# A preln attention and FP4 feed-forward kernel: the down projection one step later, two key blocks joined in one, other orders at both ends

## The chip, the cores and the metric

The kernel runs on one core of a Trainium2 chip. The time is what the device needs for one execution, in microseconds; a kernel's time is the median of its runs. Beside the runs there is one profiled execution, from which all rows come. Engines: PE is TensorE, PEld its weight loads, DVE is VectorE, ACT is ScalarE, POOL is GpSimd, SP issues most DMAs.

## The reference

Eight sequences of 2048 rows with 256 features go through one block of a transformer, all in fp32:

```python
x = x + attention(layernorm(x), W_Q, W_K, W_V)
x = x + ffn(layernorm(x), w_gate, w_up, w_down)

# attention: Q = xpos(X @ W_Q); K = xpos(X @ W_K, downscale=True); V = X @ W_V
p = softmax(Q @ K.T, axis=-1) * 0.9 ** abs(n - m)
out = p @ V
# ffn (704 hidden features); every operand of a product is rounded to FP4
# in blocks of 16, with a scale of max(abs(block)) / 6
h = silu(fp4(x) @ fp4(w_gate).T) * (fp4(x) @ fp4(w_up).T)
out = fp4(h) @ fp4(w_down).T
```

The softmax runs over all 2048 keys. The decay makes what is far from the diagonal negligible, so the kernel multiplies only a band of keys with V.

## The kernel before

**Tiles.** A row block has 128 rows. There are 16 to a sequence (NB) and 128 in all (`total`). Four row blocks are a group: it is normalised, turned, and projected to K, Q and V at a time (`project_rotated`, `rotate`, `project_v`, `keep_v`). The four groups of the first sequence are projected ahead of the steps, all others during the steps of the sequence before.

**Attention of a row block.** `scores` makes two tiles `s` of 1024 keys each in PSUM; `maximum` and `exponentials` make the softmax's numerators. `turn_p` transposes those of the band: VectorE transposes squares of 32, ScalarE's queue issues a DMA to DRAM (`there_p`), SP's queue issues four DMAs back (`runs`). `decays` multiplies by the decay on VectorE, four key blocks of 128 keys at a time, into `p_t`, and `attend` multiplies with V, one matmul for each key block. The band reaches BAND = 7 blocks to either side, so a row block has 8 to 15 key blocks. The matmuls are in fp32, and the profile lists each as two passes.

**Feed-forward of a row block.** `add_residual` and `normal_scales` make `xq`, the FP4 rounding of the rows (`Fp4.largest`, `normalize`, `round`). Its wide operations go to POOL unless `wide_on` says otherwise. `turn_xq` and `keep_xq` turn it into `xq_t`, `gate_up` multiplies, `hidden` makes `h`, which is rounded in the same way. `turn_h` (by DRAM, as above; in the last four blocks by TensorE) and `keep_h` (a ScalarE copy) turn it into `h_t`, `down` multiplies with w_down's columns into `d`, and `finish` adds and writes out.

**Order.** The program is written out by hand: each engine's queue and SP's run in the order in which `step(n)` calls these functions. In step n stand the scores of block n, `attend` of n-1, `xq` and `gate_up` of n-2, `h` of n-3 and the down part of n-4. So `keep_h(n-4)` and `down(n-4)` are in the same step, and `h_t` has one buffer. The tiles `s`, `gate`, `up`, `pp_*`, `pv` and most `pt_*` share three PSUM buffers; `d`, `o` and `pt_xq` share two.

**Both ends.** FFN weights are rounded and turned inside the early steps, by the table `IN_STEPS` (`round_weights`, `turn_ffn_weights`); key "r" is what w_gate and w_up have beyond 512 rows, ("d", 0) and ("d", 1) are the halves of w_down. Near the end the blocks in `deferred` (120 to 122) leave out their `down`; it runs among the last chains, where little else is left. In those steps `decays_first` puts `decays` ahead. After step 127 the last chains of `h` are written out by hand.

Of the kernel before, what the change touches and what calls it, by code (L numbers as in the profile page):

```python
# [34 lines left out]
def preln_xpos_retention_fp4_ffn_kernel(  # L35
# [89 lines left out]
    make_identity(nc, ident)  # L125
    neg_half = cpool.tile([P, BPG], F32, name="neg_half")
# [20 lines left out]
    load_pair("k", w_k)  # L147
    load_group(1)
# [17 lines left out]
    class Fp4:  # L166
# [37 lines left out]
        def round(self, wide_on=None):  # L204
# [19 lines left out]
            wide_on = wide_on or self.wide_on  # L224
            wide_on.tensor_tensor(v, v, big, ALU.add)  # L225
            wide_on.tensor_tensor(v, v, big, ALU.subtract)  # L226
            wide_on.tensor_tensor(self.v3, self.v3, self.wide(self.scale), ALU.mult)
# [108 lines left out]
    def round_weights(key):  # L336
        weight_fp4[key].round(nc.vector if key == ("d", 1) else None)
# [7 lines left out]
        (1, "residual"): [(round_weights, "r")],  # L345
        (2, "decays"): [(round_weights, ("d", 0)), (round_weights, ("d", 1))],
        (2, "attend"): [(turn_ffn_weights, "r")],
        (3, "maximum"): [(turn_ffn_weights, ("d", 0))],
        (3, "attend"): [(turn_ffn_weights, ("d", 1))],
# [10 lines left out]
    def statistics(k, blocks=range(BPG)):  # L360
        xt, n = groups[k], len(blocks)
        mv = small.tile([P, BPG, 2], F32, tag="mv4", bufs=2, name=f"mv_{k}_{blocks[0]}")
        for j, c in enumerate(blocks):
            st = small.tile([P, 6], F32, tag="st", name=f"st_{k}_{c}")
            nc.vector.bn_stats(st, xt[:, c, :])
            nc.vector.bn_aggr(mv[:, j, :], st)
        normed[k, blocks] = (mv, layernorm_scale(mv, n, f"a{k}_{blocks[0]}"))
# [60 lines left out]
    def rotate(k, name):  # L428
# [4 lines left out]
        for half in range(2):  # L433
            rot = act_p.tile([P, GROUP], F32, tag="rot", bufs=2, name=f"rot_{name}{half}_{k}")
# [30 lines left out]

    deferred = {n: None for n in range(total - 8, total - 5)}
# [76 lines left out]

    def decays(n):
        keys, pt = band(n), turned[n]
        p_t = prob_p.tile([P, 2 * BAND + 1, P], F32, tag="p_t", bufs=1, name=f"p_t_{n}")
        d0 = keys[0] - n % NB + BAND
        for c in range(0, len(keys), BPG):  # L550
            to = min(c + BPG, len(keys))
            nc.vector.tensor_tensor(  # L552
                p_t[:, c:to, :].rearrange("p k (a i) -> p k a i", a=NSQ),
                pt[:, c:to],
                decay_sb[:, d0 + c : d0 + to, :].rearrange("p k (a i) -> p k a i", a=NSQ),
                ALU.mult,
            )
# [4 lines left out]
    def attend(n):  # L562
# [3 lines left out]
        for j, k in enumerate(keys):  # L566
            nc.tensor.matmul(  # L567
                po,
                p_t[:, j, :],
                vt[b, k // BPG][:, k % BPG, :],  # L570
                start=(j == 0),
                stop=(j == len(keys) - 1),
            )
# [7 lines left out]
    def add_residual(n):  # L581
        if n in deferred:
            deferred[n] = act_p.tile([P, 2 * GROUP], F32, tag="kt", bufs=2 * NG, name=f"deferred_{n}")
            x1 = deferred[n][:, FC * P : FC * P + H]
        else:
            x1 = ffn_p.tile([P, H], F32, tag="x1", bufs=5, name=f"x1_{n}")
# [41 lines left out]
    def gate_up(n):  # L628
        x1, xq_t = mid.pop(n)
        pss = []  # L630
        for what, w in (("gate", wg_t), ("up", wu_t)):
            ps = ps_s.tile([P, 2, GROUP], F32, tag="s", name=f"{what}_{n}")
            for hc in range(HC):
                for half in range(2):
                    nc.tensor.matmul(  # L635
                        ps[:, half, :FH],
                        xq_t[:, hc, :],
                        w[:, hc, ts(half, FH)],
                        start=(hc == 0),
                        stop=(hc == HC - 1),  # L640
                    )
# [8 lines left out]
    def hidden(n):  # L650
# [3 lines left out]
        hid[n] = (x1, h, Fp4(h, P, F, f"h{n}", wide_on=nc.vector if n == total - 1 else None))  # L654


    def turn_h(n):
        h = hid[n][1]
        if n >= total - 4:
            pt = ps_s.tile([P, FC + 2, P], F32, tag="s", name=f"pt_h_{n}")[:, :FC, :]  # L660
            for fc in range(FC):
                at = min(fc * P, F - P)
                nc.tensor.transpose(pt[:, fc, :], h[:, at : at + P], ident)  # L663
            keep_h(n, pt.rearrange("p c (a i) -> p c a i", a=NSQ))
# [3 lines left out]
    def keep_h(n, src=None):  # L668
        x1, h, _ = hid[n]
        if n in deferred:  # L670
            h_t = deferred[n][:, : FC * P].rearrange("p (c q) -> p c q", c=FC)
        else:
            h_t = ffn_p.tile([P, FC, P], F32, tag="h_t", bufs=1, name=f"h_t_{n}")
        nc.scalar.copy(  # L674
            h_t.rearrange("p c (a i) -> p c a i", a=NSQ), in_runs(h) if src is None else src
        )
        hid[n] = (x1, h_t)

    def down(n):
        x1, h_t = hid.pop(n)  # L680
# [14 lines left out]
    hold_ffn_weights()  # L695
    load_ffn_weights("g")
    load_tables()
    load_pair("q", w_q)
# [6 lines left out]
    turn_x(0)  # L705
    load_tables()
# [4 lines left out]
    separate("q")  # L711
    for g in range(NG):
# [8 lines left out]
        if g == 0:  # L721
# [9 lines left out]
            nc.sync.dma_start(decay_sb, decay)  # L731
        if g + 1 < NG:
            project_v(g)
            keep_v(g)
        if g == 0:
            normalize_on_scalar(3)
        if g == 1:
            scale_weights("r")
            round_weights("g")

    kept = []

    def decays_first(n):

        return n - 4 in deferred

    def step(n):
# [5 lines left out]
        if on(3):  # L753
            hidden(n - 3)
        if on(2):
# [3 lines left out]
        maximum(n, 0)  # L759
        weights_in_step(n, "maximum")  # L760
        scores(n, 1)
        if decays_first(n):
            turn_xq(n - 2)
            decays(n - 1)
        if on(3):
            hid[n - 3][2].normalize()
        if on(4) and n - 4 < total - 4:
            keep_h(n - 4)
        if decays_first(n):
# [181 lines left out]
```

## Time and profile before

| | us |
|---|---|
| median of 3 runs | 2883.12 |
| lowest and highest | 2882.41, 2883.24 |
| profiled execution | 2880.51 |
| its span, first to last instruction | 2878.7 |
| PE busy | 2820.6 |
| DVE busy | 2465.1 |
| POOL busy | 1417.4 |
| ACT busy | 1077.9 |

A row of the profile's groups names the line of the kernel, the engine, the operation, and what it writes and reads, with the count; after the bar stand the busy time of the group and the mean length of one in nanoseconds; after the second bar the idle time of the engine just before such an instruction, and what ended most of it. Matmuls overlap, so the mean of one is longer than what it adds. In a timeline row the first two numbers are start and length, "xN" the number of passes, and a bracket names the idle time before and what ended it. In a list of waits the three numbers are the total, the count and the longest.

### The profile page before, as it was taken

The page shows a single profiled execution, that of the slowest core. Times are in us where ns is not written, and L with a number is a line of the kernel's source. Part 1 is how long each engine was busy: PE and PEld are TensorE (multiplying, and loading weights), DVE is VectorE, ACT ScalarE, POOL GpSimd, SP SyncE. Part 2 cuts the span into 40 slices and gives each one's busy share as a digit, 9 for nine tenths or more (in the row PEclk, how much of TensorE's full clock was granted, in tenths as well). Part 3 has the DMA queues.
Part 4 walks back from the last instruction along what each step waited for, and adds up shares of the span by engine and source line. Part 5 has one row for each costly group of instructions (what it writes and reads, how often), then busy time and mean ns, then how long its engine had stood idle before and what let it go on. Part 6 is the DMA issues. An engine that isn't in the chain of part 4 may idle for free. (4 is left out here: it accounts for less than half of the span.)

```text
span 2878.7 us, 34636 instructions
## 1 busy us (share of the span) xinstructions
PE 2820.6 (98%) x9702; PEld 1835.8 (64%) x9702; DVE 2465.1 (86%) x5635; ACT 1077.9 (37%) x1665; POOL 1417.4 (49%) x1330
## 2 busy tenths in 40 slices
PE   8899999999999999999999999999999999999997
PEld 5466666666666666666666666666666666666655
DVE  7898888888888888888888888888888888888877
ACT  3243333333433434433443334343334433333331
POOL 6544545444555454554455445544555444544443
PEclk9899999999999999999999999999999999999999
DMA  5355544555455555455546554555554555345441
GB/s 189 116 159 165 170 147 139 177 174 160 143 160 167 165 158 155 150 164 170 163 143 174 163 159 149 161 154 167 156 164 149 171 167 157 116 135 153 150 124 38
DMA packets 365761, 441.97 MB, mean 154 GB/s; under 512 B 102784, under 2 KB 313088, under 8 KB 365568
## 3 DMA queue, kind: packets, MB, share of 16 engines
q1 hardware_dynamic: 307248, 263.84, 34.4%
q10 hardware_dynamic: 58320, 175.92, 16.2%
q8 instruction: 76, 1.25, 0.2%
q14 instruction: 117, 0.96, 0.1%
HBM read 246.94 MB, written 192.68 MB: 153 GB/s over the span
## 5 line engine op out<-in xcount | busy, mean ns | idle before, releaser
L479 PE MATMUL s<-kt,qt 128*128 128x512 f32 x2048 | 901.2, 592 | 4.4 <-ACT h L647 3.7
L479 PEld LDWEIGHTS s<-kt,qt 128*128 128x128 f32 x2048 | 388.3, 190 | 461.4 <-issue 422.1
L567 PE MATMUL o<-v,p_t 128*128 128x256 f32 x2944 | 659.9, 380 | 7.0 <-DVE p_t L552 7.0
L567 PEld LDWEIGHTS o<-v,p_t 128*128 128x128 f32 x2944 | 560.9, 191 | 88.3 <-DVE p_t L552 11.3
L225 POOL TENSOR_TENSOR h<-h,big_h 128x704 f32<-128x704 f32 x127 | 214.5, 1689 | 534.0 <-DVE big_h L223 533.8
L647 ACT ACT_TABLE_LOAD x126 | 161.7, 1283 | 727.5 <-DVE xq L599 472.2
L674 ACT COPY h_t<-h 128x768 f32<-128x768 f32 x121 | 100.7, 832 | 756.3 <-DMA h<-there_h 696.4
L683 PE MATMUL d<-wd_t,h_t 128*128 128x256 f32 x1500 | 350.3, 383 | 17.5 <-ACT h_t L674 16.7
L491 DVE TENSOR_REDUCE m<-s 128x1 f32<-128x1024 f32 x256 | 310.4, 1212 | 52.5 <-PE s L479 51.2
L683 PEld LDWEIGHTS d<-wd_t,h_t 128*128 128x128 f32 x1500 | 282.9, 191 | 97.3 <-ACT h_t L674 38.3
L635 PE MATMUL gate<-wg_t,xq_t 128*128 128x352 f32 x1024 | 324.4, 460 | 1.6 <-ACT xq_t L621 1.6
L635 PE MATMUL up<-wu_t,xq_t 128*128 128x352 f32 x1024 | 324.2, 459 | 0.3 <-DVE rot_k L436 0.3
L512 ACT ACTIVATE p<-s,nmax 128x1024 f32<-128x1024 f32 x256 | 283.0, 1110 | 16.5 <-DVE nmax L496 15.0
L199 POOL TENSOR_TENSOR h<-h,inv_h 128x704 f32<-128x704 f32 x127 | 176.2, 1387 | 224.8 <-DVE inv_h L197 157.1
L635 PEld LDWEIGHTS up<-wu_t,xq_t 128*128 128x128 f32 x1024 | 194.2, 190 | 109.8 <-ACT p L512 1.3
L199 POOL TENSOR_TENSOR xq<-xq,inv_x 128x256 f32<-128x256 f32 x127 | 79.0, 622 | 359.8 <-DVE inv_x L197 116.4
L635 PEld LDWEIGHTS gate<-wg_t,xq_t 128*128 128x128 f32 x1024 | 194.0, 190 | 91.6 <-ACT xq_t L621 3.6
L552 DVE TENSOR_TENSOR p_t<-runs,decay_sb 128x512 f32<-128x512 f32 (+3 forms) x414 | 239.7, 636 | 3.1 <-issue 0.4
L243 DVE STREAM_TRANSPOSE sq_p<-p 128x1024 f32<-128x1024 f32 (+7 forms) x239 | 224.2, 973 | 10.2 <-ACT p L512 10.2
L226 POOL TENSOR_TENSOR h<-h,big_h 128x704 f32<-128x704 f32 x127 | 213.8, 1683 | 10.0
L512 ACT ACT_TABLE_LOAD x125 | 160.4, 1283 | 114.0 <-DVE nmax L496 90.3
L225 POOL TENSOR_TENSOR xq<-xq,big_x 128x256 f32<-128x256 f32 x127 | 92.3, 727 | 197.2 <-DVE big_x L223 197.2
(167 smaller groups left out, 3501.8 us busy)
## 6 DMA issues: line engine op xcount, KB each, us to landing
there_h<-sq_h ACTq DMA_DIRECT2D x124, 384.0 KB, 4.5
h<-there_h SPq DMA_DIRECT2D x496, 96.0 KB, 2.3
rope_k<-in_rope_dram SPq DMA_DIRECT2D x32, 512.0 KB, 5.8
rope_q<-in_rope_dram SPq DMA_DIRECT2D x32, 512.0 KB, 6.0
xr<-in_L_attn_X_dram SPq DMA_DIRECT2D x128, 128.0 KB, 2.2
there_xq<-sq_xq ACTq DMA_DIRECT2D x126, 128.0 KB, 1.7
xq<-there_xq SPq DMA_DIRECT2D x504, 32.0 KB, 1.7
out_dram<-x SPq DMA_DIRECT2D x125, 128.0 KB, 5.3
```

Of the source, the lines that this page charges most:

```text
L199: self.wide_on.tensor_tensor(self.v3, self.v3, self.wide(inv), ALU.mult)
L225: wide_on.tensor_tensor(v, v, big, ALU.add)
L226: wide_on.tensor_tensor(v, v, big, ALU.subtract)
L243: nc.vector.transpose(sq[:, :, at : at + w].rearrange("p c (k i) -> p k c i", i=SQ), src.rearrange("p (k c i) -> p k c i", c=NSQ, i=SQ),)
L479: nc.tensor.matmul(ps[:, j, :], q[:, dc, ts(i % BPG, P)], kt[b, half * 2 + j][:, dc, :], start=(dc == 0), stop=(dc == 1),)
L491: nc.vector.tensor_reduce(raw_scores[n][:, half : half + 1], raw_scores[n, half], AX.XY, ALU.max)
L512: nc.scalar.activation(pr, raw_scores.pop((n, half)).rearrange("p j k -> p (j k)"), AF.Exp, bias=nmax, accum_out=sums[:, half : half + 1],)
L552: nc.vector.tensor_tensor(p_t[:, c:to, :].rearrange("p k (a i) -> p k a i", a=NSQ), pt[:, c:to], decay_sb[:, d0 + c : d0 + to, :].rearrang ...
L567: nc.tensor.matmul(po, p_t[:, j, :], vt[b, k // BPG][:, k % BPG, :], start=(j == 0), stop=(j == len(keys) - 1),)
L635: nc.tensor.matmul(ps[:, half, :FH], xq_t[:, hc, :], w[:, hc, ts(half, FH)], start=(hc == 0), stop=(hc == HC - 1),)
L647: nc.scalar.activation(h[:, :F].rearrange("p (j f) -> p j f", j=2), pss[0], AF.Silu)
L683: nc.tensor.matmul(pd, h_t[:, fc, :], wd_t[:, fc, :], start=(fc == 0), stop=(fc == FC - 1))
```

## The change

Six things change together.

1. `down` and `finish` move from block n-4 to block n-5, and `h_t` gets two buffers. `keep_h(n-4)` stays in step n, but moves behind the exponentials and `keep_xq`. The deferred blocks and `decays_first` go: all blocks take the regular order.
2. Where the band has all 15 key blocks (`whole`: two row blocks in a sequence), only the lower half of its first key block and the upper half of its last are used. Their two halves are put in one block: `join_values` copies the halves of V on ScalarE, `decays` multiplies the halves of `p` into one block, and `attend` makes 14 matmuls instead of 15.
3. The program begins with 24 transposes of the identity on TensorE, into a tile that nobody reads. W_Q's load is issued earlier. Some of the normalisation of groups 3 and 4 and the rounding of w_gate change places.
4. Steps 0 to 5 are rearranged: "r" is rounded in step 2, w_down's halves are rounded in steps 3 and 4 (before, both in step 2) and turned in steps 4 and 5; step 2's projections come before "r" is turned; the second half's wide operations go to POOL instead of VectorE.
5. In the last 14 steps (`late`) `gate_up` is issued ahead of `turn_h`.
6. The last chains have another order; the wide operations on `h` of the last three blocks, not only of the last, are on VectorE; the last `h` is scaled and turned in two pieces.

```diff
+    idle = ps_s.tile([P, HALF, P], F32, tag="s", name="idle")
+    for j in range(3 * HALF):
+        nc.tensor.transpose(idle[:, j % HALF, :], ident, ident)
...
     load_pair("k", w_k)
+    load_pair("q", w_q)
     load_group(1)
...
-        weight_fp4[key].round(nc.vector if key == ("d", 1) else None)
+        weight_fp4[key].round()
...
-        (1, "residual"): [(round_weights, "r")],
-        (2, "decays"): [(round_weights, ("d", 0)), (round_weights, ("d", 1))],
+        (2, "maximum"): [(round_weights, "r")],
         (2, "attend"): [(turn_ffn_weights, "r")],
-        (3, "maximum"): [(turn_ffn_weights, ("d", 0))],
-        (3, "attend"): [(turn_ffn_weights, ("d", 1))],
+        (3, "maximum"): [(round_weights, ("d", 0))],
+        (4, "maximum"): [(turn_ffn_weights, ("d", 0))],
+        (4, "exponentials"): [(round_weights, ("d", 1))],
+        (5, "maximum"): [(turn_ffn_weights, ("d", 1))],
...
+    def whole(n):
+        return BAND <= n % NB < NB - BAND
+
+    def join_values(n):
+        b, i = divmod(n, NB)
+        v = small.tile([P, H], F32, tag="v_ends", bufs=1, name=f"v_ends_{n}")
+        for k, half in ((i - BAND, slice(P // 2, P)), (i + BAND, slice(0, P // 2))):
+            nc.scalar.copy(v[half], vt[b, k // BPG][half, k % BPG, :])
+        ends_of[n] = v
...
+        if whole(n):
+            decay_blocks(p_t, pt, 0, 0, 1, -BAND, slice(P // 2, P))
+            decay_blocks(p_t, pt, 0, 2 * BAND, 1, BAND, slice(0, P // 2))
...
+        values = [(j, vt[b, k // BPG][:, k % BPG, :]) for j, k in enumerate(keys)]
+        if whole(n):
+            values = values[1:-1] + [(0, ends_of.pop(n))]
...
-        hid[n] = (x1, h, Fp4(h, P, F, f"h{n}", wide_on=nc.vector if n == total - 1 else None))
+        hid[n] = (x1, h, Fp4(h, P, F, f"h{n}", wide_on=nc.vector if n >= total - 3 else None))
...
-            h_t = ffn_p.tile([P, FC, P], F32, tag="h_t", bufs=1, name=f"h_t_{n}")
+            h_t = ffn_p.tile([P, FC, P], F32, tag="h_t", name=f"h_t_{n}")
...
 def step(n):
...
-        if on(4) and n - 4 < total - 4:
-            keep_h(n - 4)
...
         maximum(n, 1)
         exponentials(n)
+        if n == 0:
+            normalize_on_scalar(NG)
...
+        if on(2):
             keep_xq(n - 2)
+        if on(4):
+            keep_h(n - 4)
...
-        if on(1) and n != 2 and not decays_first(n):
+        if on(1) and n not in (2, 3):
             decays(n - 1)
...
-        if on(4) and n - 4 not in deferred:
-            down(n - 4)
+        if on(5):
+            down(n - 5)
         if n == 2:
             attend(n - 1)
+            project()
             weights_in_step(n, "attend")
-            project()
...
+        if whole(n):
+            join_values(n)
...
-        if on(4) and n - 4 not in deferred:
-            finish(n - 4)
+        if on(5):
+            finish(n - 5)
...
+        late = n > total - NB + 1
+        if late:
+            gate_up(n - 2)
         if on(3) and n < total - 1:
             turn_h(n - 3)
...
-        if n == 1:
+        if n in (1, 2):
             decays(n)
...
-        if on(2):
+        if on(2) and not late:
             gate_up(n - 2)
```

The chains behind step 127, after the change (z = 127):

```python
add_residual(z); turn_h(z - 3); finish(z - 4); mid[z - 1][2].round(); turn_xq(z - 1)
normal_scales(z); mid[z][2].round(); gate_up(z - 1); hidden(z - 2); turn_xq(z); down(z - 3)
hid[z - 2][2].largest(); hid[z - 2][2].normalize(); gate_up(z); hid[z - 2][2].round()
turn_h(z - 2); hidden(z - 1); finish(z - 3)
hid[z - 1][2].largest(); hid[z - 1][2].normalize(); down(z - 2); hid[z - 1][2].round()
turn_h(z - 1); finish(z - 2); hidden(z); hid[z][2].largest(); hid[z][2].normalize(); down(z - 1)
half = FC // 2 * P // QBLK
hid[z][2].round(pieces=[slice(0, half), slice(half, F // QBLK)])
finish(z - 1); turn_h(z); down(z); finish(z)
```

## The prediction

> **What bounds the kernel now.** I read the page first, then TensorE's waits, then its timeline where it idles.
>
> ```profile
> span 2878.7 us, 34636 instructions
> PE 2820.6 (98%) x9702; PEld 1835.8 (64%) x9702; DVE 2465.1 (86%) x5635; ACT 1077.9 (37%) x1665; POOL 1417.4 (49%) x1330
> L567 PE MATMUL o<-v,p_t 128*128 128x256 f32 x2944 | 659.9, 380 | 7.0 <-DVE p_t L552 7.0
> L683 PE MATMUL d<-wd_t,h_t 128*128 128x256 f32 x1500 | 350.3, 383 | 17.5 <-ACT h_t L674 16.7
> ```
>
> TensorE is the bound: it lacks 58.1 us of the span. Passes overlap, so one costs busy time over count: an `o` pass 659.9/2944 = 0.224 us, a block's twelve `d` passes 2.6 us.
>
> ```profile
> PE d L683 <- ACT h_t L674: 16.7, 23, 2.5
> PE pp_k L417 <- ACT p L512: 7.9, 1, 7.9
> PE pt_h L663 <- POOL h L227: 7.4, 1, 7.4
> PE o L567 <- DVE p_t L552: 7.0, 4, 3.5
> PE pt_x L392 <- DVE x L372: 6.2, 1, 6.2
> PE s L479 <- ACT h L647: 3.7, 3, 1.2
> ```
>
> These waits (total, times, longest) are nearly all there is to win, apart from passes at a low clock:
>
> ```profile
> 9.46 5.72 PE L417 MATMUL pp_k<-xnt,wk_pair 128*128 128x512 f32 x8 [1.16 <-ACT xnt L394]
> 32.20 3.70 PE L417 MATMUL pp_k<-xnt,wk_pair 128*128 128x512 f32 x8 [1.49 <-ACT xnt L394]
> 96.22 6.71 PE L417 MATMUL pp_k<-xnt,wk_pair 128*128 128x512 f32 x8 [7.89 <-ACT p L512]
> 123.78 7.44 PE L567 MATMUL o<-v,p_t 128*128 128x256 f32 x20 [3.50 <-DVE p_t L552]
> 2793.34 4.58 PE L567 MATMUL o<-v,p_t 128*128 128x256 f32 x20 [1.64 <-DVE p_t L552]
> 2863.52 1.54 PE L663 MATMUL pt_h<-ident,h 128*128 128x128 f32 x6 [7.40 <-POOL h L227]
> 2866.01 5.07 PE L683 MATMUL d<-wd_t,h_t 128*128 128x256 f32 x12 [0.94 <-ACT h_t L674]
> ```
>
> Eight projection passes take 3.60 or 3.70 us when warm, but 5.72 at the start and 6.71 after a 7.89 us gap; twenty `o` passes 4.58, but 7.44 after 3.50. So a long gap is paid again: 2.1 + 3.1 + 2.9 us. After gaps of 1.2 to 1.7 nothing is lost. The busy times by stretch (TensorE, weight loads, VectorE, ScalarE, POOL, then the granted clock) say the same:
>
> ```profile
> 90.00:100.00 10.00, 3.78 (x5) 1.72 (x6) 8.52 (x12) 4.83 (x11) 5.22 (x5) 0.60 0.23 68
> 120.00:130.00 10.00, 6.50 (x17) 5.00 (x17) 7.95 (x18) 4.29 (x7) 4.57 (x3) 0.66 0.20 68
> ```
>
> **Joined blocks.** `whole(n)` holds at two of 16 row blocks of a sequence, 16 in all; each loses one key block, two passes: 16 x 2 x 0.224 = 7.2 us off TensorE. VectorE: three key blocks in a 384-wide multiply (0.550) become a 128-wide one (0.324) and two on 64 partitions, at most 0.324 each: +0.42 a time, beside TensorE's longest steps. ScalarE gets two copies of 64x256 (nearest, the 128x256 `xq_t` copy: 0.398), 0.8 us at 37% load. Behind them stand `there_h`'s issue and the silu, but both already come after the `attend` that the second join waits for. Bounds: 7.2 if covered, 16 x 0.8 - 7.2 = 5.6 lost if ScalarE's copies stood on the path. I take 7.2 won.
>
> **Down one step later.** 19 of the 23 waits lie in regular steps: eleven before 2450 us (5.4 us) and eight between 2560 and 2720 (6.1). The copy `keep_h` (0.83) still runs in step n, now behind the exponentials and `xq_t`, and `d` of that block is wanted a step later, so these vanish. What is late next is `p_t`: around 2607 its multiplies end at 2609.6 and `o` begins at 2609.8; without the wait TensorE would be there at 2608.7, when the first of three is done. I take 10.0 of 11.5 (bounds 4 and 11.5). On SP, `finish` stands where it was, writing one block older.
>
> **First steps.** Two parts. Before step 0 (43.5 us): warm first `pp_k`, 5.72 to 3.60, is 2.1; x of group 3 is normalised on ScalarE after `xnt` of group 2, which takes away the 1.49. W_Q's load passes ahead of x of group 1 on SP, 256 KB at the 247 GB/s of the first 10 us, 1.1 us: that x is then normalised at 15.0 instead of 13.9, and `pt_x` wants it at 16.6 (9.46 + 3.6 + 3.6), so free. Step 0 could begin at 39.9.
>
> Steps 0 to 4 (43.5 to 157.1, 113.6 us): by the busy times VectorE works 97.3 us and TensorE 100.9, 6.0 of it slow clock. Taking out that, one `d` and one `pt_wd` (both now in step 5), TensorE needs 100.9 - 6.0 - 2.6 - 0.7 = 91.6. The stretch will be between 91.6 and 110.3 (113.6 less the moved work). I walked it with these rows:
> - Step 0: w_gate's rounding (1.16 + 1.86 + 0.69 on VectorE) is now right before the first maximum, so `nmax` comes at 51.5 against 51.88; the second `pp_q` needs the buffer that exp frees, 52.8 against 53.8. Of the 3.6 only 1.0 is left.
> - Step 1: `moments` (2.3) went ahead of step 0, and `normalize_on_scalar` of group 4 (3.6 on ScalarE) to step 0, where `there_p`'s issue behind it waits for VectorE until 60 anyway. The remainder's rounding leaves step 1, so `p_t` of step 1, three multiplies of 5.09 beside POOL's rounding, costs 1.9: ready at 78.3 against 86.7.
> - Step 2: w_down's two roundings (10.3 on VectorE, 1.88 for 0.53 in places) are gone, exp comes at 84.3 against 94.97, `turn_p` follows it at once (its issue on ScalarE ahead of the `xq_t` copy, its four loads on SP ahead of the rope tables, which are wanted a step later), and `pp_k` no longer queues behind `pt_wr`: the 7.89 wait goes, and its slow passes.
> - Step 3: w_down's first half (2.0 on VectorE, 4.8 on POOL) stands ahead of `hid` and `xq`: `xq_t` at 113.2, TensorE waits 3.5.
> - Step 4: its second half comes before `decays`, `p_t` at 133, TensorE waits 5 there and runs slow afterwards.
>
> So step 5 starts at 143.3, 13.8 earlier. Step 4's `p_t` runs beside POOL's rounding, as the 5.09 did, not 1.9 to 2.3: 2.8 back. I take 11.0; bounds 3.3 (only the moved work) and 25.5 (39.9 + 91.6 against 157.1).
>
> Two buffers for `rot` became three: a wait of 0.61 on VectorE before step 1 that nobody follows; nothing.
>
> **Warm-up, weighed.** No row shows whether transposes alone bring the clock up. [...]
>
> **Last chains.** From step 124 on (2745.95) the kernel takes 132.75 us. Step 124 has no `d` and takes 17.08 without waits; each later step has two `o` passes less. With their three `d` back, steps 124 to 126 cost TensorE (17.08 + 16.63 + 16.18) + 7.8 = 57.7 against 57.3 now: the waits on the silu (1.21 + 1.22) and on `p_t` (1.64 + 1.64) pay for them. They go since `gate_up` stands ahead of `turn_h` in the `late` steps: the silu no longer queues on ScalarE behind `there_h`'s issue, which waits for VectorE; that issue in turn comes 2 us later, a step before it is needed.
>
> From step 127 (2803.24) to the end is 75.5. The last three blocks go through VectorE one after the other. One costs hidden 0.89, largest 0.88, six small 1.6, then 0.89 + 0.88 + 0.53 + 0.53 + 3 x 0.89 = 8.8. Before, POOL did the wide operations of two of them and the chain took 2836.6 to 2866.1, 29.5, with 1.87 for 0.53 while both engines worked; then 12.6 more, as `d` of block 126 (5.07, slow) stood before the last. After: 3 x 8.8 + 2 x 0.42 = 27.3, then half of `pt_h` (0.2), of the copy (0.4), three key chunks of `d` (0.7 to 2.5), the add (0.4) and the write (2.7): 5.5. The gain is 2.2 + 7.1 = 9.3, also since the 7.40 wait was for POOL. Less 0.4 for the three steps: 8.9, bounds 5 and 11.
>
> **The sum.** 7.2 + 10.0 + 11.0 + 8.9 = 37.1. Against the profiled execution's 2880.5 (span 2878.7) this is 2843.4; the median of the runs lies 2.6 above it: 2846.
>
> **Rivals.**
> - The warm-up doesn't warm: 5.72 stays, 2.1 at most, since step 0 is VectorE's; 2848. For it, only short transposes would run; against it, the wait of 6.17 is filled.
> - First steps stay VectorE's: it is 86% busy over 43.5 to 157.1 and all its work but 2 us is still there. Only the moved work is won, 7.7 less: 2854.
> - The waits on `h_t` come back as waits on `p_t`: 10.0 lost, 2856. For it, VectorE's 86 to 90% in the 100 us windows; against it, only four waits on `p_t` in the run.
> - Slower: `keep_h`'s 0.83 now stands on ScalarE ahead of the copies of V, which free a PSUM tile. If TensorE had to wait for that tile, each of the 56 half copies would cost 0.83: 46 us, 2892. It decides once ScalarE is some 7 us later in a step than now (`runs` lands that long before `p_t` is worked on); against it, 37% load, and that ScalarE waits 696 us for the very data in the place it had.
>
> **Chances.** Forecast 0.50, warm-up 0.15, first steps 0.15, `p_t` 0.10, slower 0.05; 0.05 for several shortfalls together, 0.03 of it so many that the time stays within 0.2% (5.8 us, about what a measurement of this kernel can tell). Faster 0.92, same 0.03, slower 0.05. Range: from 2835 (7 of the 14.5 us more that the bound of the first steps allows, 2.1 in the last chains, 1.5 in the down waits) to 2862 (shortfalls of 16).
>
> **What would show it.** Right: `d` waits on `h_t` only in the last 50 us; `o` with 2912 passes; no `pp_k` wait at 96; first `pp_k` 3.6; waits on `xq_t` and `p_t` of 3 to 5 in steps 3 and 4; from the last `s` to the end 66 us. Wrong: waits on `p_t` spread over the run, or TensorE waiting for copies of V or `xnt`.

## The result and the profile after

The changed kernel takes 2857.64 us (median, 2856.16 to 2858.3) against 2883.05 for the kernel before: a ratio of 0.9912, interval 0.9894 to 0.9929. It is 25.4 us faster. The forecast was 2846 (37 faster), the range 2835 to 2862. The profiled execution took 2857.39.

The page's first lines and its two groups that were shown of before:

```profile
span 2855.6 us, 34236 instructions
PE 2812.5 (98%) x9694; PEld 1836.5 (64%) x9694; DVE 2478.9 (87%) x5673; ACT 1077.9 (38%) x1698; POOL 1408.4 (49%) x1325
L603 PE MATMUL o<-v,p_t 128*128 128x256 f32 x2880 | 644.3, 380 | 3.7 <-DVE p_t L573 3.5
L715 PE MATMUL d<-wd_t,h_t 128*128 128x256 f32 x1536 | 356.3, 382 | 1.8 <-ACT h_t L705 1.8
```

TensorE still lacks 43.1 us of the span (58.1 before). `d` has all but lost its waits (17.5 to 1.8). The 32 passes on `v_ends` are a group of their own, so `o` has 2880 + 32 = 2912.

TensorE's waits after (total, times, longest):

```profile
PE gate L665 <- ACT xq_t L649: 10.7, 3, 9.1
PE pp_q L432 <- ACT p L523: 6.3, 1, 6.3
PE pt_h L695 <- DVE h L233: 6.2, 2, 3.9
PE pt_wd L317 <- ACT h L677: 4.2, 1, 4.2
PE o L603 <- DVE p_t L573: 3.5, 4, 2.3
```

Three of the first four are each one long wait, or little more than one, in the first steps. Its timeline shows where:

```profile
8.74 3.70 PE L432 MATMUL pp_k<-xnt,wk_pair 128*128 128x512 f32 x8 [1.16 <-ACT xnt L409]
56.70 5.29 PE L432 MATMUL pp_q<-xnt,wq_pair 128*128 128x512 f32 x8 [6.29 <-ACT p L523]
91.54 3.60 PE L432 MATMUL pp_k<-xnt,wk_pair 128*128 128x512 f32 x8
126.62 5.06 PE L665 MATMUL gate<-wg_t,xq_t 128*128 128x352 f32 x8 [9.11 <-ACT xq_t L649]
145.63 5.60 PE L603 MATMUL o<-v,p_t 128*128 128x256 f32 x22 [2.30 <-DVE p_t L573]
163.64 1.51 PE L317 MATMUL pt_wd<-ident,wd_rows 128*128 128x128 f32 x6 [4.25 <-ACT h L677]
2836.36 1.51 PE L695 MATMUL pt_h<-ident,h 128*128 128x128 f32 x6 [3.87 <-DVE h L233]
2838.76 4.34 PE L715 MATMUL d<-wd_t,h_t 128*128 128x256 f32 x12 [0.89 <-ACT h_t L705]
2847.64 4.93 PE L715 MATMUL d<-wd_t,h_t 128*128 128x256 f32 x12
```

The first `pp_k` is warm (3.70, was 5.72) and the 7.89 before `pp_k` at 96 is gone, but new waits of 6.29, 9.11, 2.30 and 4.25 have come. After the 6.29, the 9.11 and the 4.25 the passes are slow and the granted clock is low: 0.66 between 50 and 60 us, 0.57 between 120 and 130, 0.66 between 160 and 170 (eight `gate` passes take 5.06; without a gap 2.53). After the 2.30 the granted clock is 1.00 (145 to 155 us); there `o` takes 5.60 because it follows the `p_t` multiplies, of which the last ends at 149.61.

Read by where the scores of a step begin, the gain falls into four stretches:

| kernel | step 0 | step 1 | step 6 | step 6 to 124 | step 127 to end |
|---|---|---|---|---|---|
| before | 43.50 | 58.10 | 179.28 | 2566.7 | 75.5 |
| changed | 39.95 | 62.70 | 184.71 | 2546.2 | 67.6 |

Up to step 6 the change **loses** 5.4 us, from there to step 124 it gains 20.5, in steps 124 to 126 0.3, and from step 127 on 7.9: 23.1 before rounding, the difference of the two spans. The question for the runs is thus the first steps: 11.0 were to be gained there.

### The profile page after: what moved, and what is told of

Same layout as the page of the kernel before. It is cut to its first block, busy times and chain, and to the rows that moved or that the text cites. A ratio compares the mean times of both kernels' runs of the same rounds, so it can differ in the third digit from the quotient of the medians.

```text
span 2855.6 us, 34236 instructions
## 1 busy us (share of the span) xinstructions
PE 2812.5 (98%) x9694; PEld 1836.5 (64%) x9694; DVE 2478.9 (87%) x5673; ACT 1077.9 (38%) x1698; POOL 1408.4 (49%) x1325
## 3 DMA queue, kind: packets, MB, share of 16 engines
q8 instruction: 76, 1.25, 0.2%
## 5 line engine op out<-in xcount | busy, mean ns | idle before, releaser
L603 PE MATMUL o<-v,p_t 128*128 128x256 f32 x2880 | 644.3, 380 | 3.7 <-DVE p_t L573 3.5
L603 PEld LDWEIGHTS o<-v,p_t 128*128 128x128 f32 x2880 | 545.8, 190 | 84.3 <-DVE p_t L573 9.5
L229 POOL TENSOR_TENSOR h<-h,big_h 128x704 f32<-128x704 f32 x125 | 211.3, 1690 | 524.0 <-DVE big_h L228 524.0
L715 PE MATMUL d<-wd_t,h_t 128*128 128x256 f32 x1536 | 356.3, 382 | 1.8 <-ACT h_t L705 1.8
L715 PEld LDWEIGHTS d<-wd_t,h_t 128*128 128x128 f32 x1536 | 294.1, 192 | 71.9 <-issue 29.2
L665 PE MATMUL gate<-wg_t,xq_t 128*128 128x352 f32 x1024 | 327.0, 462 | 10.8 <-ACT xq_t L649 10.7
L523 ACT ACTIVATE p<-s,nmax 128x1024 f32<-128x1024 f32 x256 | 282.8, 1110 | 26.9 <-DVE nmax L507 25.4
L573 DVE TENSOR_TENSOR p_t<-runs,decay_sb 128x512 f32<-128x512 f32 (+1 forms) x446 | 244.2, 601 | 9.7 <-DMA runs<-there_p 5.5
L230 POOL TENSOR_TENSOR h<-h,big_h 128x704 f32<-128x704 f32 x125 | 210.3, 1683 | 9.8
L233 POOL TENSOR_TENSOR h<-h,scale_h 128x704 f32<-128x704 f32 x125 | 173.4, 1388 | 9.8
```

The source lines that it names most:

```text
L229: self.wide_on.tensor_tensor(v, v, big, ALU.add)
L230: self.wide_on.tensor_tensor(v, v, big, ALU.subtract)
L233: self.wide_on.tensor_tensor(self.v3[:, k], self.v3[:, k], wide[:, k], ALU.mult)
L523: nc.scalar.activation(pr, raw_scores.pop((n, half)).rearrange("p j k -> p (j k)"), AF.Exp, bias=nmax, accum_out=sums[:, half : half + 1],)
L573: nc.vector.tensor_tensor(p_t[rows, at : at + w, :].rearrange("p k (a i) -> p k a i", a=NSQ), pt[rows, of : of + w], decay_sb[rows, d + BA ...
L603: nc.tensor.matmul(po, p_t[:, j, :], v, start=(j == values[0][0]), stop=(j == values[-1][0]))
```

## The experiments

Each run was compared with the kernel before on its own chip; these medians lie between 2880.3 and 2883.1, so times are given as ratios to them (0.001 is 2.9 us; the changed kernel has 0.9912). What an edit does inside the kernel is read from where the steps begin, in one profiled execution each. The stretch from step 6 to step 124, where the edits of e1 to e4 and e7 to e12 change nothing, comes out at 2543.8 to 2547.2: so much do profiled executions differ there. At the start of step 6 they differ too: e5 and e7, whose first steps are those of the changed kernel, get there at 185.0 and 182.1 (changed kernel 184.7), so 3 us at that point tell nothing. The theory (A): POOL's rounding of the weights, now lying beside VectorE's small operations, holds these up. The rival (B): the order alone does it.

**e1: w_down's three POOL operations left out.**

```diff
+            if not wide_too:
+                return
             self.wide_on.tensor_tensor(v, v, big, ALU.add)
...
-        weight_fp4[key].round()
+        weight_fp4[key].round(wide_too=key not in (("d", 0), ("d", 1)))
```

> The changed kernel without the three wide operations that POOL does on each half of w_down (add, subtract, scale; w_down then goes into the multiplication unrounded). Everything else, VectorE's part of that rounding too, stays in its place. Theory A (POOL's rounding of the weights stretches the VectorE operations beside it, and what hangs on them comes late): in step 3 the small operations of h go from 1.4 to 1.7 us back to about 0.2 each, the three p_t multiplies of step 4 from 4.72 to about 1.6; TensorE's wait on xq_t goes from 9.1 to about 4, the 2.3 on p_t and the 4.2 before pt_wd go; step 6's scores begin at 170 to 175 instead of 184.7; time 2843 to 2850 against 2857.6. Theory B (the order itself costs it: the xq_t copy stands behind two exponentials, pt_wd stands between the two halves of the scores): the waits stay within 2 us of what they are, time 2854 to 2858.

Ratio 0.9891 (0.9876 to 0.9906). From step 1 to step 6 it takes 112.4 us (64.88 to 177.32) instead of 122.0: 9.6 less. (e5, e7 and e9, which leave those steps as they are, take 120.0, 118.9 and 120.3, so 6.4 to 9.6 is what can be said.) VectorE's operations on h's scales in step 3, and the three `p_t` multiplies of step 4, in the timeline of the changed kernel:

```profile
114.90 1.68 DVE L198 SCALAR_TENSOR_TENSOR res_h<-sixth_h,amax_h 128x44 f32<-128x44 f32 x1
116.62 1.71 DVE L199 SCALAR_TENSOR_TENSOR res_h<-sixth_h,res_h 128x44 f32<-128x44 f32 x1
118.43 1.36 DVE L200 SCALAR_TENSOR_TENSOR scale_h<-res_h,sixth_h 128x44 f32<-128x44 f32 x1
120.39 0.39 DVE L249 STREAM_TRANSPOSE sq_xq<-xq 128x256 f32<-128x256 f32 x1
144.89 4.72 DVE L573 TENSOR_TENSOR p_t<-runs,decay_sb 128x512 f32<-128x512 f32 x3
```

and without POOL's operations:

```profile
115.57 0.20 DVE L198 SCALAR_TENSOR_TENSOR res_h<-sixth_h,amax_h 128x44 f32<-128x44 f32 x1
115.81 0.20 DVE L199 SCALAR_TENSOR_TENSOR res_h<-sixth_h,res_h 128x44 f32<-128x44 f32 x1
116.05 0.20 DVE L200 SCALAR_TENSOR_TENSOR scale_h<-res_h,sixth_h 128x44 f32<-128x44 f32 x1
116.85 0.39 DVE L251 STREAM_TRANSPOSE sq_xq<-xq 128x256 f32<-128x256 f32 x1
141.18 1.75 DVE L575 TENSOR_TENSOR p_t<-runs,decay_sb 128x512 f32<-128x512 f32 x3
```

Three operations go from 4.75 to 0.60 us, the multiplies from 4.72 to 1.75. TensorE's wait on `xq_t` falls from 9.1 to 4.9, that before `pt_wd` from 4.2 to 1.8, so A holds for what lies beside POOL. But e1 also takes POOL's work itself away (4.7 us on the first half, 5.7 on the second), so its gain is not that of the overlap alone. Two parts of its expectation fell: the 2.30 on `p_t` stayed (it is for the first multiply, which stands behind VectorE's own part of w_down's rounding), and step 6 came at 177.3, not at 170 to 175.

**e2: w_gate's rounding back in the projection loop.**

```diff
         if g == 1:
             scale_weights("r")
+            round_weights("g")
...
     deviations(NG)
-    round_weights("g")
```

> The changed kernel with w_gate's rounding put back inside the loop of the first projections (g == 1, behind the scales of the remainder) instead of right before step 0. Theory A: POOL's three operations no longer lie beside the small operations of w_down in step 0, which go from 2.0 to 2.2 back to about 0.2 us; the first nmax moves from 55.2 to about 50 to 52, TensorE's wait before the second pp_q from 6.3 to below 3.6 and its slow passes (5.29) to 3.7 to 4.5; time 2852 to 2856. Theory B (step 0 is set by the amount of VectorE work, wherever it stands): what is saved in step 0 is paid before it, step 0 begins 2 to 4 us later than 39.95 and the second pp_q stays at 55 to 57; time within 1.5 us of 2857.6.

Ratio 0.9900 (0.9887 to 0.9914). Step 0 begins at 40.21, as in the changed kernel, and step 1 at 57.84 instead of 62.70: step 0 takes 17.6 us instead of 22.8. The wait of 6.3 is gone. That is A, and more than A expected of it: the three VectorE operations of that rounding (3.7 us) found room before step 0 too. At step 6 it is 4.7 us ahead of the changed kernel (180.0). How the operations are held up shows when VectorE's and POOL's rows of step 0 in the changed kernel stand side by side:

```profile
47.40 0.88 DVE L190 TENSOR_REDUCE amax_wd<-wd_rows 128x44 f32<-128x704 f32 x1
48.30 0.58 DVE L197 TENSOR_SCALAR sixth_wd<-amax_wd 128x44 f32<-128x44 f32 x1
48.92 0.20 DVE L198 SCALAR_TENSOR_TENSOR res_wd<-sixth_wd,amax_wd 128x44 f32<-128x44 f32 x1
49.16 2.23 DVE L199 SCALAR_TENSOR_TENSOR res_wd<-sixth_wd,res_wd 128x44 f32<-128x44 f32 x1
51.42 1.98 DVE L200 SCALAR_TENSOR_TENSOR scale_wd<-res_wd,sixth_wd 128x44 f32<-128x44 f32 x1
```

```profile
46.49 2.36 POOL L229 TENSOR_TENSOR wg_rows<-wg_rows,wbig 128x1024 f32<-128x1024 f32 x1
48.92 2.40 POOL L230 TENSOR_TENSOR wg_rows<-wg_rows,wbig 128x1024 f32<-128x1024 f32 x1
51.41 1.93 POOL L233 TENSOR_TENSOR wg_rows<-wg_rows,wd_rows 128x1024 f32<-128x1024 f32 x1
```

The operation that began at 49.16 ended at 51.39, POOL's at 51.32; the next ended at 53.40, POOL's at 53.34. Each of these two VectorE operations with two SBUF inputs, 0.20 us long in e2, where w_gate's POOL operations are not beside it, lasts to the end of the POOL operation beside it (0.07 and 0.06 us apart); one, at 48.92, where POOL's next also begins, took its 0.20. The reduction at 47.40, with one input, took its usual 0.88 beside POOL. But the TENSOR_SCALAR behind it, also with one input, was held up as well: 0.58 instead of 0.19, until 48.88, where POOL's operation had ended at 48.85. So two inputs are not the only case; what decides for operations with one, no run here was made to tell. By what means one engine holds the other up, no row shows.

**e3: w_down's halves rounded behind the output multiplications.**

```diff
-        (3, "maximum"): [(round_weights, ("d", 0))],
-        (4, "maximum"): [(turn_ffn_weights, ("d", 0))],
-        (4, "exponentials"): [(round_weights, ("d", 1))],
-        (5, "maximum"): [(turn_ffn_weights, ("d", 1))],
+        (3, "attend"): [(round_weights, ("d", 0))],
+        (4, "exponentials"): [(turn_ffn_weights, ("d", 0))],
+        (4, "attend"): [(round_weights, ("d", 1))],
+        (5, "decays"): [(turn_ffn_weights, ("d", 1))],
```

> The changed kernel with w_down's first half rounded behind the output multiplications of step 3 instead of in the middle of its scores, its second half behind those of step 4 instead of behind the exponentials, and the transposes of the second half behind step 5's scores, ahead of the down multiplication, instead of between the two halves of the scores. Theory A: h and xq are no longer beside w_down's POOL operations, so TensorE's wait on xq_t goes from 9.1 to 3 to 5, and the 2.3 on p_t and 4.2 before pt_wd go; step 6's scores begin at 172 to 178 instead of 184.7, time 2845 to 2851. Theory B (order): only the 4.2 before pt_wd and the slow clock after it (2 to 3) go, the wait on xq_t stays at 7 to 9; time 2850 to 2854. Against both: the roundings now lie beside the residual and the next step's xq, and as much is lost there; time 2856 to 2860.

Ratio 0.9935 (0.9923 to 0.9948), with an interval that just overlaps the changed kernel's; step 6 at 189.0, 4.3 later: the case against both. The wait on `xq_t` did fall to 3.1, as A has it, but TensorE's waits are now others:

```profile
PE pp_q L432 <- ACT p L523: 6.3, 1, 6.3
PE pv L464 <- ACT p L523: 6.0, 1, 6.0
...
PE pt_wd L317 <- ACT p L523: 5.1, 1, 5.1
PE gate L665 <- ACT xq_t L649: 4.6, 3, 3.1
PE d L715 <- ACT wd_t L319: 3.3, 1, 3.3
```

`pt_wd` takes one of the three large PSUM tiles; behind the scores its turn, and that of `pv` after it, comes only when the exponentials have read the scores. So the place of these six transposes matters as much as that of the rounding: the order (B) has a part.

**e4: the first steps in the order of before, all else new.** w_gate's rounding is in the loop as in e2; the body of steps 0 to 3 is again that of before, VectorE again does the second half's wide operations, and the table of the weights' steps is that of before:

```diff
+        (1, "residual"): [(round_weights, "r")],
+        (2, "decays"): [(round_weights, ("d", 0)), (round_weights, ("d", 1))],
+        (3, "maximum"): [(turn_ffn_weights, ("d", 0))],
+        (3, "attend"): [(turn_ffn_weights, ("d", 1))],
```

> The changed kernel with the weights' rounding and the order of steps 0 to 4 as they were in the kernel before (w_gate in the projection loop, the remainder at the end of step 1, both parts of w_down in step 2, the second on VectorE). Warm-up, loads, joined blocks, down one step later and the last chains stay new. If the new order of the first steps is what lost time (before: step 6 at 179.3 with one down multiplication and a later step 0; after: 184.7): step 0 begins at 40 to 41.5, the 7.9 wait before pp_k in step 2 comes back, step 6 begins at 172 to 177, time 2845 to 2851. If the loss comes from another part (the joined blocks or the later down): step 6 begins at 182 to 187, time 2855 to 2860.

Ratio 0.9888 (0.9874 to 0.9901). Step 0 at 40.49, step 1 at 58.12, the 7.9 before `pp_k` is back, and step 6 begins at 177.6: 7.1 us earlier than in the changed kernel (expected 172 to 177). So the new order of the first steps, w_gate's place included, is what loses, and it is worth less than nothing: with the warm-up, the loads and one `d` less ahead of step 6, e4 is there 1.7 us ahead of before, and the new order takes 7.1. Most of that is w_gate's place: e2, which changes nothing else, has 4.7 of it, and the 2.4 between e2 and e4 lie within what executions differ by. The two orders differ inside the steps, though. Step 5 takes 28.9 us in the changed kernel, 22.2 before and 23.5 in e4; in all runs in which w_down's second half is turned in step 5 it takes 25.8 to 38.0.

**e5: key blocks not joined.**

```diff
     def whole(n):
-        return BAND <= n % NB < NB - BAND
+        return False
```

> The changed kernel with the key blocks not joined (whole() is never true). Theory (32 passes fewer in every sequence pair of middle blocks, covered everywhere): from step 6's scores to step 124's it takes 2546.2 us in the changed kernel and 2553.4 here (7.2 more), time 7.2 us above the changed kernel's. Rival (the narrower multiplies on VectorE and the copies on ScalarE eat a part of it): 2 to 4 us more. Rival (they cost more than the passes): the time falls.

Ratio 0.9928 (0.9915 to 0.9940). Step 6 to step 124 takes 2550.1 us: 3.9 more than in the changed kernel. Compared in the fourteen steps past step 9 that hold a joined `o`, it is 310.0 against 304.5, 0.39 a step, thus 6.3 for the sixteen (7.2 forecast). The 3.9 lies where the rival had it, but the whole stretch differs by 3.4 between executions; the fourteen steps take 304.0 to 305.3 in every other run whose regular steps are those of the changed kernel, so the 310.0 stands out by 4.7 to 6.0, and that decides for the theory with a little less than 7.2. The other steps of the stretch take 2240.0 here, 2239.9 to 2242.1 in those runs. The copies of `v_ends` cost 0.403 us each (0.398 forecast), and TensorE waits for none of them.

**e6: down four steps behind again.**

```diff
-        if on(5):
-            down(n - 5)
+        if n == 5:
+            down(0)
+            finish(0)
+        if on(5):
+            down(n - 4)
...
```

`keep_h` also stands ahead of the `xq` transposes again.

> The changed kernel with down, finish and keep_h back at four steps behind, keep_h again ahead of the xq transposes (blocks 0 and 1 both come down in step 5, since w_down is only ready then). Theory (the later down won the 19 waits on h_t, 11.5 us): such waits come back, some 20 of them with 0.3 to 0.9 us each, and the stretch from step 6 to step 124 grows from 2546.2 to 2556 to 2558. Rival (they were won by something else, such as an earlier start of POOL's or VectorE's chain): fewer than eight such waits, the stretch grows by less than 4 us.

Ratio 0.9981 (0.9972 to 0.9989). The waits are back, and step 6 to step 124 takes 2560.3, 14.1 more. The waits of the whole run, and the `d` passes of that stretch alone, in e6 and in the changed kernel:

```profile
PE d L715 <- ACT h_t L705: 16.2, 27, 1.4
```

```profile
L715 PE MATMUL d<-wd_t,h_t 128*128 128x256 f32 x1416 | 328.4, 381 | 13.2 <-ACT h_t L705 12.9
L715 PE MATMUL d<-wd_t,h_t 128*128 128x256 f32 x1416 | 324.9, 379 | 0.0
```

The later `down` is worth more than the 11.5 us of waits which it was to remove, and the two rows say why. In that stretch the waits on `h_t` take 12.9 us, and the same 1416 passes of `d` are also busy for 3.5 us longer when they have to wait. Less the other waits of the changed kernel there (2.8, on the silu and on `p_t`), which e6 does not have, this makes 13.6 of the 14.1. The kernel before shows the same: 11.0 of waits in the stretch, and `d` busy for 328.3. 14.1 and e5's 6.3 make 20.4; the stretch gained 20.5 from before to after.

**e7: the last chains' wide operations on POOL.**

```diff
-        hid[n] = (x1, h, Fp4(h, P, F, f"h{n}", wide_on=nc.vector if n >= total - 3 else None))
+        hid[n] = (x1, h, Fp4(h, P, F, f"h{n}", wide_on=nc.vector if n == total - 1 else None))
```

> The changed kernel with the wide operations of the rounding of blocks 125 and 126 on POOL, as before; block 127's stay on VectorE. From step 127's scores to the end the changed kernel takes 67.6 us. Theory (in the last chains the two engines wait for each other, a VectorE operation with two SBUF inputs ending when POOL's operation ends): operations of 0.53 to 0.89 us on VectorE become 1.4 to 1.9 beside POOL's, and the stretch is 69.5 to 72. Rival (POOL takes work off the engine that sets the end): 64 to 67.

Ratio 0.9903 (0.9889 to 0.9916). From step 127 to the end: 66.4 us, within the 64.7 to 67.6 that kernels with the unchanged end show. The theory's 69.5 to 72 did not come; the number lies in the rival's range, but no gain is shown either. VectorE is freed of four operations a block, yet held up beside POOL again (its 0.19 and 0.20 become 1.66 and 1.27) and waits 1.6 twice for POOL's multiply; by the total, the two about cancel. The operation that went from 0.19 to 1.66 is again one with a single SBUF input.

**e8: the weights' rounding and turning replaced once more.** With w_gate as in e2, the xq transposes of step 3 ahead of h's `normalize`, and block 0's `down` and `finish` at the end of step 5.

```diff
+        (3, "exponentials"): [(round_weights, ("d", 0))],
         (4, "maximum"): [(turn_ffn_weights, ("d", 0))],
+        (4, "attend"): [(round_weights, ("d", 1))],
+        (5, "attend"): [(turn_ffn_weights, ("d", 1))],
...
+        if n == 3:
+            keep_xq(n - 2)
         exponentials(n)
```

> The changed kernel with w_gate's rounding back in the loop of the first projections; w_down's first half rounded in step 3 behind the exponentials (after the small operations of h and the transposes of xq); in step 3 the xq transposes ahead of h's small operations and the xq_t copy ahead of the exponentials; the second half rounded behind the output multiplications of step 4 and turned behind those of step 5, block 0's down multiplication at the end of step 5. Theory A (what VectorE's two-input operations wait for is POOL's operation beside them, and three places in the order carry it on to TensorE): the waits of 6.3 on p, 9.1 on xq_t, 4.2 before pt_wd and 2.3 on p_t all fall below 2 us; step 6's scores begin at 160 to 169 instead of 184.7; time 2835 to 2843 on the scale where the changed kernel has 2857.6. Theory C (VectorE's amount of work sets the first steps): the waits move elsewhere and step 6 begins at 173 to 180; time 2846 to 2853.

Ratio 0.9888 (0.9873 to 0.9903). The wait on `xq_t` in step 3 is 1.6, that on `p_t` in step 4 0.5, and step 4 begins at 118.9 instead of 133.9. Then 6.4 of these 15.0 us are lost again: step 6 is at 176.1, 8.6 earlier. Theory A's 160 to 169 thus did not come; step 6 and the time lie where C had them. But VectorE's amount of work is not what sets them: from step 0 to step 6 it is busy for 115.1 of 135.8 us and idle for 20.7. TensorE's new waits:

```profile
127.70 1.51 PE L317 MATMUL pt_wd<-ident,wd_rows 128*128 128x128 f32 x6 [5.18 <-ACT h L677]
153.17 6.05 PE L490 MATMUL s<-kt,qt 128*128 128x512 f32 x8 [4.33 <-ACT h L677]
```

TensorE waits for the gate's PSUM tile, which the silu frees; the silu stands on ScalarE behind `there_h`. For the first of these waits POOL rounds that h only after w_down's half. Ahead of the second it rounds h first; there VectorE's two TENSOR_SCALAR operations on w_down, held beside POOL (1.88 and 1.59 for 0.53), stand ahead of the transposes of h. The next run but one, e10, takes the silu away from there.

**e9: no transposes at the start.**

```diff
-    idle = ps_s.tile([P, HALF, P], F32, tag="s", name="idle")
-    for j in range(3 * HALF):
-        nc.tensor.transpose(idle[:, j % HALF, :], ident, ident)
```

> The changed kernel without the 24 transposes of the identity at its start. Theory (they bring the clock up): the first pp_k takes 5.5 to 6 us instead of 3.70 for eight passes, step 0's scores begin at 41.5 to 43.5 instead of 39.95. Rival (transposes don't count for the clock, the faster first pp_k comes from elsewhere): it stays at 3.6 to 3.8. In time both give between 0 and 3 us more, since step 0 is set by VectorE.

Ratio 0.9904 (0.9888 to 0.9921); the time doesn't tell the two apart. The first `pp_k`, and step 0's start at 42.37 instead of 39.95, do:

```profile
9.13 6.67 PE L429 MATMUL pp_k<-xnt,wk_pair 128*128 128x512 f32 x8 [1.16 <-ACT xnt L406]
```

6.67 without the transposes (5.5 to 6 expected), 3.70 with them. That this is the clock is the author's estimate from the lengths of the passes: from 0 to 20 us the granted clock reads 1.00 in the changed kernel, and also in the kernel before, where the first `pp_k` took 5.72. Of the 2.4 us only 1.0 is left at step 6, less than executions differ by.

**e10: e8 with the silu ahead of there_h in steps 3 and 4.**

```diff
-        late = n > total - NB + 1
+        late = n > total - NB + 1 or n in (3, 4)
```

> The kernel with the weights replaced (e8), and in steps 3 and 4 gate_up ahead of turn_h, so that the silu stands ahead of there_h's issue on ScalarE. Theory (the silu waits behind that issue, for an h that POOL rounds only after w_down's half, and with it the PSUM tile of the gate): the 5.2 before pt_wd and the 4.3 before the second scores of step 5 fall below 1 each; step 6's scores begin at 163 to 169 (e8: 176.1), time 7 to 12 us below e8's 2848.9. Rival (VectorE is full there): the waits go over to p_t or xq_t, step 6 at 172 to 176, time within 4 of e8's.

Ratio 0.9888 (0.9873 to 0.9903), step 6 at 177.4: the rival. The waits on the silu are below 1, and in their place TensorE waits for VectorE, which reads the `up` tile next:

```profile
PE o L603 <- DVE p_t L573: 5.2, 5, 3.6
PE s L490 <- DVE h L683: 4.7, 1, 4.7
PE pv L464 <- DVE h L683: 3.4, 1, 3.4
```

VectorE isn't full there, though: it is idle for 22.0 of the 137.1 us from step 0 to step 6. The longest single piece is in step 4, up to the transposes of h, for which POOL's rounding of h comes late behind w_down's:

```profile
123.31 1.04 DVE L249 STREAM_TRANSPOSE sq_h<-h 128x640 f32<-128x640 f32 x2 [3.01 <-POOL h L233]
```

As these waits read, w_down's 4.7 to 5.7 us a half on POOL reach TensorE by another way each time.

**e11 and e12: two other places for the second half, and the clock at the end.** Both are e10 with one round_weights line moved ((5, "exponentials"), turned at the end of step 5, and (4, "decays")); e12 also has transposes of the identity ahead of the last two `pt_h`.

> As the run with the silu ahead, but w_down's second half rounded in step 5 behind the exponentials and turned at the end of that step, right before block 0's down multiplication. Theory: POOL is free in step 4, so that rstd_f and xq of block 3 come up to 4 us earlier, the wait on p_t in step 5 falls below 1; in step 5 pt_wd and d wait up to 3 us instead. Time within 3 us of the run with the silu ahead; it tells only which place is better.

> As the run with the silu ahead, but w_down's second half rounded behind the p_t multiplies of step 4, ahead of h's rounding, and transposes of the identity put into TensorE's waits of 3.9 and 2.3 us ahead of the last two pt_h (24 and 16). If short transposes hold the clock up: the last two d take 2.6 to 2.9 us instead of 4.3 and 4.9, and from step 127's scores to the end it takes 64 to 65 us instead of 66.3 to 67.6. If not: 4.3 to 5, and 66 to 68. The place of the second half is worth within 3 us either way, read at step 6's start.

e11: ratio 0.9911 (0.9896 to 0.9926), step 6 at 185.3; `o` waits 6.1 for `p_t`, `d` 5.4 for `wd_t`. e12: 0.9898 (0.9884 to 0.9913), step 6 at 181.7, of which some 2 us are slow passes in step 0 that its edit doesn't touch (step 1 at 60.0, e10 57.9). Neither place is better than e10's; e11's is 7.9 us worse, more than expected. At the end of e12:

```profile
2833.12 0.85 PE L695 MATMUL pt_h<-ident,h 128*128 128x128 f32 x6 [1.25 <-DVE h L233]
2834.85 2.86 PE L715 MATMUL d<-wd_t,h_t 128*128 128x256 f32 x12 [0.89 <-ACT h_t L705]
...
2842.20 0.52 PE L695 MATMUL pt_h<-ident,h 128*128 128x128 f32 x3 [2.75 <-DVE h L233]
2843.35 0.55 PE L695 MATMUL pt_h<-ident,h 128*128 128x128 f32 x3 [0.62 <-ACT h_t L705]
2843.73 4.44 PE L715 MATMUL d<-wd_t,h_t 128*128 128x256 f32 x12
```

The filler made block 126's `d` warm (2.86; 4.86 in e10, 4.34 in the changed kernel), without a gain at the end; the second filler ended 2.75 before `h` was there, and the last `d` was slow (4.44) again. The end stayed at 66.5 us (66.3 in e10).

## Why the prediction was right and where it was wrong

The direction and the range held; the forecast missed by 11.6 us. That the range held was in part luck: two of the four terms came out beyond their own bounds, `down` above and the first steps below, and the first made up for a part of the second. Term by term, from the positions and the runs:

| term | forecast | measured | from |
|---|---|---|---|
| joined blocks | 7.2 | 6.3 | e5 |
| down one step later | 10.0 (4 to 11.5) | 14.1 | e6 |
| first steps | 11.0 (3.3 to 25.5) | -5.4 | start of step 6 |
| last chains | 8.9 (5 to 11) | 8.1 | steps 124 to end |
| sum | 37.1 | 23.1 | spans |

**Down.** The mechanism was right: e6 brings the waits back. The size was not: I took the waits less something for `p_t`; only 0.9 of waits on `p_t` lies in that stretch after the change. And I took the waits alone, where the `d` passes behind them also lose 3.5 us (324.9 busy in the changed kernel, 328.3 before and 328.4 in e6). The rival of waits on `p_t` had nothing, and the slower one neither: no wait for a copy of V appears.

**Last chains.** The sum was right, one of its reasons not: 2.2 of the 9.3 were to come from VectorE working alone. By e7, POOL or VectorE makes no difference that stands out from the 64.7 to 67.6; what the split last block and block 127's order in the end gave was not separated. The 67.6 of the changed kernel is at the upper end of what the same chains take in other runs, so the term may be up to 2.9 larger.

**First steps.** Here the walk failed. It had 11.0 won, and 5.4 were lost: 16.4 too little. By where the steps begin, 5.6 of these are in step 0, 4.1 in steps 1 to 4, and 6.7 in step 5, where the walk no longer went.
- "Step 0: nmax comes at 51.5". It came at 55.20. I added w_gate's three VectorE operations and left the small operations of w_down's scales behind them at 0.20, although POOL's three of 1.9 to 2.4 us now lay beside them. Two of them took 4.2 together. Of the 3.6 by which step 0 begins earlier, the walk left 1.0 at the start of step 1; measured, step 1 begins 4.6 later than before, behind a wait of 6.29. e2 gives 5.1 for the place of this rounding.
- "Step 3: w_down's first half stands ahead: `xq_t` at 113.2, TensorE waits 3.5". The walk added 2.0 on VectorE and 4.8 on POOL, but again not that h's small operations lie beside POOL's. They took 4.75 for 0.60, so the squares of xq were ready at 120.4, the copy came behind the exponentials at 126.2 and TensorE waited 9.11. In step 4 the wait on `p_t` was 2.30, not 5, and the clock stayed up (1.00 between 145 and 155 us).
- Step 5 was not walked: the stretch ended where it begins, and the `pt_wd` that was taken out of it (0.7) had only moved behind that end. There step 5 takes 28.9 us for 22.2. `pt_wd` needs the PSUM tile that the silu frees, and the silu comes late: in step 4 the `p_t` multiplies beside POOL hold VectorE until 149.61, h's rounding behind them starts at 151.86 on VectorE and at 153.95 on POOL, and the silu ends at 163.50. The stretched multiplies were priced (as the 5.09 of before), but only as a wait for `o`. `pt_wd` waits 4.25, and slow passes follow.

How much of the 10.8 beyond step 0 is POOL's overlap alone is not separated: e1's 6.4 to 9.6 also contains POOL's own work. The row which should have told me was in my own text: `p_t` took 5.09 beside POOL and 1.9 without, and an operation on w_down 1.88 for 0.53. I used that for the one multiply and not for the other operations that came to lie beside POOL. The first steps' rival (VectorE keeps them) saw that this term could fail, at 2854, but for another reason: in e8 and e10 VectorE is idle for 20.7 and 22.0 us of the first steps, in part waiting for POOL.

**The signs.** Right: `d` waits only in the last 50 us; 2912 passes of `o`; first `pp_k` 3.70; no `pp_k` wait at 96; 67.6 from the last scores to the end (66 forecast). Wrong: the waits on `xq_t` and `p_t` were 9.1 and 2.3, not 3 to 5 each.

**Warm-up.** The step was right, and its rival wrong: 6.67 without the transposes and 3.70 with them. The granted clock reads 1.00 over them (0 to 8 us in the changed kernel); by what they do this, no row shows. The 2.4 us are still there where step 1 begins (65.40 in e9, 62.70 in the changed kernel); at step 6, 1.0 is left.

**What stays open.** Four arrangements of the first steps (e1, which leaves work out, e4, e8, e10) end at step 6 within 1.5 us of each other, 176.1 to 177.6, each with other waits. e4, e8 and e10 have a ratio of 0.9888: some 7 us under the changed kernel by step 6's start, though the intervals of the times overlap. From step 0 to step 6, e4, e8 and e10 take 135.8 to 137.1 us; the kernel before took 135.8, with one `d` more. So no new order won anything inside these steps, and what is ahead at step 6 is the earlier start. Whether some order gets below that, these runs don't tell.

## What to carry to other kernels

When a step of work is moved, list what will lie beside it on the other engines, and price those operations too: here the moved operations cost about what was expected, and the short ones beside them cost up to eleven times their own length (2.23 us for 0.20). The moved work's whole chain counts (VectorE's part, POOL's queue, the turn on TensorE with its PSUM tile, the copies), and each of these can bring the wait back at another place. Walk on past the end of the stretch: work that has moved behind it looks won. Read a gain by where the steps begin, stretch by stretch: one total of 25 us hid a loss of 5 and gains of 20 and 8.

## What the hardware showed that was not expected

- Five VectorE operations with two SBUF inputs lasted until POOL's operation beside them ended: 128x44 elements in 2.23 and 1.98 us (step 0) and in 1.68, 1.71 and 1.36 (step 3) for 0.20, ends 0.05 to 0.07 us apart, while a reduction took 0.88 beside POOL (0.89 in e7 with POOL idle). Some operations with one input took longer beside POOL too: a TENSOR_SCALAR of 128x44 took 0.58 and, in e7, 1.66 for 0.19, one of 128x704 in e8 1.88 for 0.53.
- 24 transposes of the identity in 4.76 us let the first projection run at 3.70 us (6.67 without them); in e12, after a gap of 2.75 us behind a later filler, the last `d` took 4.44 (the one before it, after a gap of 1.25 behind the filler, 2.86).
- The same 1416 passes of `d` are busy for 328.4 us in e6, where they wait 22 times for `h_t`, and for 324.9 in the changed kernel, where they never wait: 3.5 us more, beside the 12.9 of idle time that is listed for the waits.
